# A graph network layer on one core: a step's second four gathers get one more wait, and a sign change moves to GpSimd

## Chip, core and metric

The kernel runs on 1 core of a Trainium2 chip. The metric is the device time of one execution in microseconds (us); the time of a kernel is the median of its runs. Engine names in the profile: PE is TensorE (matmul), PEld its weight loads, DVE is VectorE, ACT is ScalarE, POOL is GpSimd, SP is the engine that here only issues DMAs.

## What is computed

The reference is one message-passing layer over 6250 nodes of 128 values and 100000 edges, sorted by destination:

```python
row, col = (edge_index[0], edge_index[1])
msg_in = jnp.concatenate([node_features[row], node_features[col]], axis=-1)
h = jax.nn.relu(msg_in @ Wm1 + bm1)
h = jax.nn.relu(h @ Wm2 + bm2)
messages = h @ Wm3 + bm3
agg = jax.ops.segment_sum(messages, col, num_segments=num_nodes)
count = jax.ops.segment_sum(jnp.ones(...), col, num_segments=num_nodes)
agg = agg / jnp.clip(count, 1.0)[:, None]
node_in = jnp.concatenate([node_features, agg], axis=-1)
upd = jax.nn.relu(node_in @ Wn1 + bn1) @ Wn2 + bn2
return node_features + upd          # then layernorm(x + this)
```

## The kernel before

It has three stages, which the trace tells apart.

The preparation (to about 90 us) turns `x` and multiplies it by the two halves of `Wm1`. This gives two tables in HBM: `atab` (one row for each source node, float32, `a_table`) and `btab` (one row of three bf16 terms for each destination node, `b_table`). It works through 13 blocks of nodes; PE, ACT, POOL and SP run in the order written, and DVE from some point on too. The row `nb2` holds the second layer's bias on all partitions: POOL's queue loads it (line 190), and DVE changes its sign (line 433). Line 553 needs it so: relu(z + b) is taken as max(z, -b), with b added back later.

The edge loop (about 91 to 1630 us) takes two groups of 512 edges in each of 98 steps (`NP`). It is a software pipeline. Its order in step i on PE is:

- `turned` (line 580) transposes the sums of step i-4, and DVE's `add_up` (line 590) adds them to `acc`;
- `first_layer` of p = i-1 (lines 529 and 536) brings the gathered rows and the one-hot picked destination rows into PSUM (`ph`); ACT applies relu (line 542, four instructions);
- `sums` of step i-3 (line 561) sums messages over destinations in two banks, and ACT copies them to `part` (line 569, two instructions, `part_of`);
- `second_layer` of step i-2 (line 551) makes 32 matmuls into four banks, and DVE takes the max with `nb2` out of each (line 553, four instructions).

The PSUM pool `p2` has four banks. `turned` takes two, `sums` two, `second_layer` four, so `turned` of the next step needs the first two banks of `second_layer` freed by DVE's line 553.

The step's inputs come through a tile `rows`, of which there are two buffers. `fetch` (line 480) fills one for step i+1 while the other is in use: eight indirect gathers of 128 rows from `atab` on POOL's queue (line 488, four for each group), and eight window loads from `btab` on SP's queue (line 494). The buffer of step i+1 is that of step i-1, so the first gather waits for the end of `first_layer` of step i-1, which runs in step i. The later seven follow it in POOL's queue. The destinations `db` are loaded by ACT's queue (line 384, two DMAs a step), which stand behind the two copies of line 569 in ACT's order.

The node stage (from about 1638 us) divides by the counts, applies the last two layers and normalizes.

Of the kernel before, what the change touches and what calls it, by code (L numbers as in the profile page):

```python
# [9 lines left out]
F32 = mybir.dt.float32  # L10
# [3 lines left out]
ALU = mybir.AluOpType  # L14
# [5 lines left out]
P = 128  # L20
# [7 lines left out]
def kernel(  # L28
# [36 lines left out]
    nc = tc.nc  # L65
    N, D = x.shape
    E = src.shape[0]
    H = wm1.shape[1]
    HC = H // P
    GT = 4  # L70
# [19 lines left out]
    srcT = const.tile([P, NG, GT], I32, name="srcT")  # L90
# [51 lines left out]
    nb2 = const.tile([P, 1, H], F32, name="nb2")  # L142
# [5 lines left out]
    ld = edge.enter_context(tc.tile_pool(name="ld", bufs=4, side="right"))  # L148

    with tc.tile_pool(name="prep", bufs=1) as prep, tc.tile_pool(  # L150
        name="brow", bufs=6
    ) as brow, tc.tile_pool(name="pp", bufs=3, space=PSUM) as pp, tc.tile_pool(
        name="pb", bufs=5, space=PSUM
# [7 lines left out]
        with tc.high_priority():  # L161
# [6 lines left out]
            def load_x(b0, b1, behind=None):  # L168
                t0, t1 = 4 * b0, 4 * b1
                if behind is not None:  # L170
                    nc.vector.tensor_copy(x_sb[:, t0, :1], xT[:, behind * 4 * P:behind * 4 * P + 1])
                nc.sync.dma_start(x_sb[:, t0:t1, :].rearrange("p (b i) d -> p b i d", i=4), xb[:, b0:b1])
# [89 lines left out]
        def a_table(t0):  # L262
            m = min(2, NT - t0)
            pbt = products(t0, m, 0)
            rows = brow.tile([P, 2, H], F32, name="at", bufs=7)
            nc.scalar.copy(rows[:, :m], pbt[:, :m])
            nc.sync.dma_start(rows_of(atab, t0, m), rows[:, :m])
# [33 lines left out]
        def turn(t0):  # L301
            m = min(4, NT - t0)
            w = min(m * P, N - t0 * P)
            pt = pp.tile([P, 4 * P], F32, name="pt", tag="pp")
            for i in range(m):
                n = min(P, w)
                nc.tensor.transpose(pt[:, i * P:i * P + n], x_sb[:n, t0 + i, :], ident[:n, :n])
            nc.scalar.copy(xT[:, t0 * P:t0 * P + w], pt[:, :w])
# [97 lines left out]
        for i in range(BLOCKS):  # L406
            if i in X_LOADS:
                load_x(*X_LOADS[i], behind=i)
                if X_LOADS[i][1] == BLOCKS - 1:
                    nc.sync.dma_start(x_sb[:N - NTF * P, NTF, :], x[NTF * P:, :])  # L410
            for n, t0 in enumerate(range(4 * i, min(4 * i + 4, NT), 2)):

                if n == (i == 0) and i + 1 < BLOCKS:
                    turn(4 * i + 4)
                a_table(t0)
            b_stores()
            for _ in range(min(len(blank), 3 if i < BEHIND else 1)):
                nc.gpsimd.memset(blank.pop(0), 0.0)
            if i == BEHIND + 1:
                weights(i)  # L420
            if i == INDICES:
                starts()
            if i - INDICES in (1, 2):
                columns(i - INDICES - 1)
                partition_bases(i - INDICES - 1)
            if i == BLOCKS - 1:
                nc.scalar.copy(tilei, base[0:1].rearrange("p r w -> p (r w)"))
            if i >= BEHIND:
                b_block(i - BEHIND)
            if BLOCKS - 3 <= i:  # L430
                early.append(destinations(2 * len(early), 2, dst_row))
        assert not blank
        nc.vector.tensor_scalar(nb2, nb2, -1.0, None, op0=ALU.mult)
        behind = list(X_BEHIND)
        with tc.manual_schedule(engines={ENG.DVE}):
            for n, j in enumerate(range(BLOCKS - BEHIND, BLOCKS)):
# [27 lines left out]
    with edge, tc.tile_pool(name="wk", bufs=2) as wk, tc.tile_pool(  # L464
        name="p1", bufs=1, space=PSUM
# [11 lines left out]
        def flat_bank():  # L477
            return bank().rearrange("p t h -> p (t h)")

        def fetch(groups, queues):  # L480


            rows = ld.tile([P, 2, (GT + 1) * H], F32, name="rows", bufs=2)
            got = []
            for i, ((idx, firsts), queue) in enumerate(zip(groups, queues)):
                ag = rows[:, i, :GT * H].rearrange("p (j h) -> p j h", j=GT)
                for j in range(GT):
                    nc.gpsimd.indirect_dma_start(  # L488
                        out=ag[:, j, :], out_offset=None, in_=atab[:, :],
                        in_offset=bass.IndirectOffsetOnAxis(ap=idx[:, j:j + 1], axis=0))  # L490
                bw = rows[:, i, GT * H:].bitcast(BF16).rearrange("p (k h) -> p k h", k=2)
                for j, first in enumerate(firsts):
                    terms = btab[ds(first, WB + 1)].rearrange("n c h -> (n c) h")
                    queue.dma_start(bw[j // 2 * NQ:(j // 2 + 1) * NQ, j % 2, :], terms[:NQ])
                got.append((ag, bw))
            return got
# [69 lines left out]
        def part_of(pgs, nts):  # L566
            part = wk.tile([P, 2, H + 1], F32, name="part")
            for i, (pg, nt) in enumerate(zip(pgs, nts)):
                nc.scalar.copy(part[:nt * WN, i], pg[:nt * WN, :H + 1])  # L569
            return part  # L570
# [48 lines left out]
        NP = NG // 2  # L619
        NTS = [GT if g < NGF else LT for g in range(NG)]  # L620
        st = {}
# [6 lines left out]
        def summed(p):  # L628
            s = st[p]
            return sums([(s["ohs"][i], h2s[i], s["nts"][i]) for i in range(2)])  # L630

        rest_bank = [bank]
        rest = (x for b in X_END for x in x_part(b, lambda: rest_bank[0](), (nc.scalar, nc.scalar)))
        for i in range(NP + 4):
            if i == 8:
                late_loads()

                none = wk.tile([16, (NG * GE - E) // 16 + 1], I32, name="none", bufs=1)
                nc.vector.memset(none, NONE)
                nc.sync.dma_start(dpad[E - 16:].rearrange("(p e) -> p e", p=16), none)  # L640
                nc.sync.dma_start(dpad[:E].rearrange("(p e) -> p e", p=16), dst.rearrange("(p e) -> p e", p=16))
            if i < NP:
                dbs = early.pop(0) if early else destinations(2 * i, min(2, NGF - 2 * i), dst_row)
                if 2 * i + 1 == NGF:
                    dbs = dbs + last_destinations()
                queues = [(nc.sync, ENG.SP), (nc.scalar, ENG.Activation) if i == 0 else (nc.sync, ENG.SP)]
                firsts = [load_bases(tilei[0:1, g * GT:(g + 1) * GT], NTS[g], eng)
                          for g, (_, eng) in zip((2 * i, 2 * i + 1), queues)]
                got = fetch([(srcT[:, 2 * i + k, :], firsts[k]) for k in range(2)], [q for q, _ in queues])
                st[i] = dict(nts=NTS[2 * i:2 * i + 2], got=got, dbs=dbs)  # L650
            if i == 1:
                for k in range(SLOTS):
                    nc.gpsimd.memset(acc[:, HC, k * SLOT:(k + 1) * SLOT], 0.0)
            p = i - 1
            if p < 0:
                continue
            if p == 0:
                make_hot(0)
            k = p - 3
            if k >= 0:  # L660
                firsts = [load_bases(tilei[0:1, g * GT:(g + 1) * GT], NTS[g], ENG.DVE) for g in (2 * k, 2 * k + 1)]
                pt = turned(st[k]["part"], st[k]["nts"])
                add_up(pt, firsts, st.pop(k)["nts"])
            for step, after in enumerate((10, 12, 14)):
                if i >= after and (i - after) % 4 == 0 and (i - after) // 4 < len(pieces):
                    double((i - after) // 4, step)
            if p + 1 < NP:
                make_hot(p + 1)
            if p < NP:
                s = st[p]  # L670
                s["h1"] = first_layer(s.pop("got"), s.pop("ohts"), s["nts"])
            if p < 2:
                whole(x_part(X_FIRST[p], bank, (nc.scalar, nc.vector)))
            if p - 2 == NP - 1:
                next(rest)
            if 0 <= p - 2 < NP:
                st[p - 2]["part"] = part_of(summed(p - 2), st[p - 2]["nts"])
            if p - 2 == NP - 1:
                next(rest)
            if p - 2 == NP:  # L680
                next(rest)
            if 0 <= p - 1 < NP:
                s = st[p - 1]
                for j, nt in enumerate(s["nts"]):
                    second_layer(s["h1"][:, j], h2s[j], nt)
# [7 lines left out]
        groups = nc.values_load(  # L693
            groups_i[0:1, 0:1], min_val=0, max_val=NG,
            skip_runtime_bounds_check_because="0 or the number of groups, by its computation")
        with tc.For_i(0, groups, 1) as g:
# [3 lines left out]
            with tc.For_i(0, more, 1):  # L700
# [12 lines left out]
                got = fetch([(idx, load_bases(ti, GT, ENG.SP))], [nc.sync])  # L713
# [4 lines left out]
                part = part_of(sums([(oh, h2s[0], GT)]), [GT])  # L718
# [13 lines left out]
    with tc.tile_pool(name="nd", bufs=2) as nd, tc.tile_pool(name="nr", bufs=1) as nr, tc.tile_pool(  # L732
        name="pm", bufs=4, space=PSUM
    ) as pm, tc.tile_pool(name="pu", bufs=2, space=PSUM) as pu, tc.tile_pool(
        name="po", bufs=2, space=PSUM
# [169 lines left out]
```

## Time and profile before

| what | value |
|---|---|
| runs | 1714.18, 1715.68, 1729.71 us (median 1715.68) |
| profiled execution: its own time, its span | 1716.33 us, 1714.6 us |
| busy: PE, PEld, DVE, ACT, POOL | 1338.1, 1052.5, 656.4, 381.9, 813.5 us |
| mean granted TensorE clock | 0.855 |
| gathers, line 488 | 784, 954 ns each |
| DVE line 553 | 391, 688 ns each, 958.9 us of idle before them |
| PE line 580, idle before it | 329.9 us |
| DVE's wait before line 433 | 4.0 us, for the load of `nb2` |

The busy time of an engine is the union of its instructions; the issue of DMAs on SP and ACT is not counted. A gather on POOL counts as busy while POOL makes its descriptors; its data land later. In a group's row the duration is the mean of one instruction, and what stands behind the bar is the engine's idle time just before such instructions, with what ended most of it. "remote" stands where the profile knows no instruction that ended a wait.

### The profile page before, as it was taken

What the parts mean: (1) busy time and instruction counts of PE and PEld (TensorE: products, weight loads), DVE (VectorE), ACT (ScalarE), POOL (GpSimd) and SP (SyncE); (2) the same over time, 40 slices, a digit from 0 to 9 for tenths busy, and PEclk for the clock granted to TensorE, in tenths of its full rate; (3) what the DMA queues carried; (4) which work ended last, traced back from release to release, by engine and by line L of the source; (5) the groups of instructions that cost most, each with busy time, mean ns of one, the idle gap of its engine ahead of it and who ended that gap; (6) DMA issues with size and microseconds to landing.
All of it is one profiled execution on the core that took longest, in us unless ns stands there. A gap on an engine that the chain in (4) does not pass through costs nothing. (4 is left out here: it accounts for less than half of the span.)

```text
span 1714.6 us, 32171 instructions
## 1 busy us (share of the span) xinstructions
PE 1338.1 (78%) x11212; PEld 1052.5 (61%) x11213; DVE 656.4 (38%) x2076; ACT 381.9 (22%) x773; POOL 813.5 (47%) x873
## 2 busy tenths in 40 slices
PE   8877778677778777778777777877778778777898
PEld 7556566565666556556655665656666566655756
DVE  5523323323333333323333332333333333332467
ACT  5522112122112212212211211212222112221236
POOL 7754454454454445444445444445545444544121
PEclk9888888888887888888888788888988888888899
DMA  9743344333444334334434334333434333333133
GB/s 305 256 122 105 103 108 113 101 108 100 115 111 111 104 107 116 100 106 115 112 96 118 99 94 111 99 87 110 113 95 110 95 109 101 102 100 107 34 109 111
DMA packets 167585, 193.63 MB, mean 113 GB/s; under 512 B 30906, under 2 KB 133260, under 8 KB 167404
## 3 DMA queue, kind: packets, MB, share of 16 engines
q0 software_dynamic: 38160, 103.75, 22.4%
q1 hardware_dynamic: 100492, 61.80, 12.3%
q10 hardware_dynamic: 28768, 26.01, 5.2%
q8 instruction: 89, 1.46, 0.4%
q14 instruction: 76, 0.62, 0.1%
HBM read 168.92 MB, written 22.88 MB: 112 GB/s over the span
## 5 line engine op out<-in xcount | busy, mean ns | idle before, releaser
L488 POOL DMA_INDIRECT rows<-atab,srcT x784 | 747.7, 954 | 785.0 <-PE ph L536 568.8
L551 PE MATMUL bank<-w,h 128*128 128x256 f32 x3128 | 709.9, 385 | 1.8 <-issue 1.2
L551 PEld LDWEIGHTS bank<-w,h 128*128 128x128 f32 x3128 | 592.7, 192 | 137.2 <-PE bank L561 56.9
L553 DVE TENSOR_TENSOR h<-bank,nb 128x512 f32<-128x512 f32 x391 | 254.9, 688 | 958.9 <-remote 501.0
L542 ACT ACTIVATE h<-ph,b 128x512 f32<-128x512 f32 x392 | 236.7, 686 | 1240.3 <-PE ph L536 1199.0
L580 PE MATMUL bank<-ident,part 64*128 64x64 f32 x1173 | 103.4, 290 | 329.9 <-DVE h L553 316.8
L580 PEld LDWEIGHTS bank<-ident,part 64*128 64x128 f32 x1173 | 73.7, 184 | 376.6 <-DVE h L553 335.4
L529 PE MATMUL ph<-ident,rows 64*128 64x64 f32 x3128 | 191.3, 297 | 19.5 <-issue 18.2
L529 PEld LDWEIGHTS ph<-ident,rows 64*128 64x128 f32 x3128 | 177.8, 207 | 24.7 <-issue 22.0
L590 DVE TENSOR_TENSOR acc<-acc,bank 128x63 f32 x782 | 171.8, 220 | 35.3 <-DVE acc L590 2.1
L561 PE MATMUL bank<-h,oh 128*32 128x257 f32 x1564 | 152.3, 525 | 0.2 <-ACT x_sb L358 0.2
L536 PE MATMUL ph<-oht,rows 64*128 64x128 bf16 x1564 | 106.5, 298 | 1.0 <-DMA rows<-btab 1.0
L512 DVE TENSOR_SCALAR oht<-db,pbase 128x128 bf16<-128x128 int32 x392 | 95.0, 286 | 0.1
L536 PEld LDWEIGHTS <-rows 64*128 64x128 bf16 x1564 | 91.7, 141 | 1.2 <-DMA rows<-btab 1.2
L561 PEld LDWEIGHTS bank<-h,oh 128*32 128x32 f32 x1564 | 51.5, 140 | 54.9 <-issue 28.7
L569 ACT COPY part<-bank 128x257 f32<-128x257 f32 x196 | 66.3, 399 | 12.2 <-PE bank L561 8.4
L763 POOL TENSOR_TENSOR agg<-total,rc 128x512 f32<-128x512 f32 (+2 forms) x15 | 16.0, 1070 | 86.0 <-DMA rcol<-acc 42.0
L515 DVE TENSOR_TENSOR oh<-iota_n,dloc 128x128 f32<-128x128 f32 x196 | 55.6, 284 | 0.0
L258 PE MATMUL pbt<-w,xT 128*128 128x256 f32 x196 | 46.2, 382 | 3.5 <-DVE rest L285 3.5
L258 PEld LDWEIGHTS pbt<-w,xT 128*128 128x128 f32 x196 | 36.0, 191 | 10.0 <-DVE rest L285 4.0
L786 PEld LDWEIGHTS pot<-wu,u 128*128 128x128 f32 (+1 forms) x196 | 24.0, 191 | 6.6 <-issue 4.1
L355 PE MATMUL pxu<-xT,wu 128*128 128x512 f32 x36 | 20.6, 713 | 8.0 <-DVE rest L285 8.0
(125 smaller groups left out, 427.0 us busy)
## 6 DMA issues: line engine op xcount, KB each, us to landing
rows<-btab SPq DMA_DIRECT2D x778, 32.0 KB
db<-in_dst_dram ACTq DMA_DIRECT2D x194, 128.0 KB
rows<-atab,srcT POOLq DMA_INDIRECT x784
btab<-acc SPq DMA_DIRECT2D x24, 384.0 KB
atab<-at SPq DMA_DIRECT2D x24, 256.0 KB
xd<-in_x_dram SPq DMA_DIRECT2D x12, 256.0 KB
x2tab<-xd SPq DMA_DIRECT2D x12, 256.0 KB
x_sb<-in_x_dram SPq DMA_DIRECT2D x5, 512.0 KB
```

The source lines that it names most:

```text
L258: nc.tensor.matmul(pbt[:, a, :], xT[:, (t0 + a) * P:(t0 + a + 1) * P], w1[:, k, :], start=True, stop=True)
L488: nc.gpsimd.indirect_dma_start(out=ag[:, j, :], out_offset=None, in_=atab[:, :], in_offset=bass.IndirectOffsetOnAxis(ap=idx[:, j:j + 1], a ...
L512: nc.vector.tensor_scalar(ohts[:n, i, k, :], db[:n, k * P:(k + 1) * P], pb_cols[:n, k:k + 1], None, op0=ALU.is_equal)
L529: nc.tensor.matmul(ph[:, i, h, c, u * NQ:(u + 1) * NQ], ag[halves[h], u, c * P:(c + 1) * P], ident[halves[h], halves[h]], is_transpose=Tru ...
L536: nc.tensor.matmul(ph[:, i, h, c, k * P:(k + 1) * P], bw[halves[h], k, c * P:(c + 1) * P], ohts[halves[h], i, k, :], start=False, stop=Tru ...
L542: nc.scalar.activation(h1[:, i, c, :nh * 2 * P].rearrange("p (h e) -> p h e", h=nh), ph[:, i, :nh, c, :], AF.Relu, bias=b1[:, c:c + 1])
L551: nc.tensor.matmul(ph2[:, j - j0, :], h1[:, c, j * P:(j + 1) * P], w2[:, c, :], start=(c == 0), stop=(c == HC - 1))
L553: nc.vector.tensor_tensor(h2[:, j0:j0 + 2, :H], ph2, nb2.to_broadcast([P, 2, H]), op=ALU.max)
L561: nc.tensor.matmul(pg[j * WN:(j + 1) * WN, :H + 1], oh[:, j, :], h2[:, j, :], start=True, stop=True, skip_group_check=True)
L569: nc.scalar.copy(part[:nt * WN, i], pg[:nt * WN, :H + 1])
L580: nc.tensor.matmul(pts[h][:, i, c, :], rows, ident[halves[h], halves[h]], is_transpose=True, start=True, stop=True, skip_group_check=True)
L590: nc.vector.tensor_add(window, window, pts[h][:, i, :, k:k + WB])
```

## The change

There are two edits. The sign change of `nb2` moves from DVE, behind the preparation's blocks, to POOL, in the last block. And from step 3 on, each step allocates the next step's `rows` buffer early, behind its `part_of`, and lets ACT copy four values a partition from `part` into it: the first value of each of the four rows that the second group's gathers will write. Each of these gathers writes over one of these values, so the fifth gather of the next fetch also waits for this copy (the sixth to eighth stand behind it in the queue). The copy stands in ACT's order behind line 569 and ahead of the next two loads of `db` (line 384). On PE, DVE and SP the order of the instructions stays, but for the one that leaves DVE; there are 94 such copies, from step 3 to step 96.

```diff
             if i == BLOCKS - 1:
                 nc.scalar.copy(tilei, base[0:1].rearrange("p r w -> p (r w)"))
+                nc.gpsimd.tensor_scalar(nb2, nb2, -1.0, None, op0=ALU.mult)
...
         assert not blank
-        nc.vector.tensor_scalar(nb2, nb2, -1.0, None, op0=ALU.mult)
...
-        def fetch(groups, queues):
-            rows = ld.tile([P, 2, (GT + 1) * H], F32, name="rows", bufs=2)
+        def rows_tile():
+            return ld.tile([P, 2, (GT + 1) * H], F32, name="rows", bufs=2)
+
+        def fetch(groups, queues, rows=None):
+            rows = rows_tile() if rows is None else rows
...
+        held = None
...
-                got = fetch([(srcT[:, 2 * i + k, :], firsts[k]) for k in range(2)], [q for q, _ in queues])
+                got = fetch([(srcT[:, 2 * i + k, :], firsts[k]) for k in range(2)], [q for q, _ in queues], held)
+                held = None
...
             if 0 <= p - 2 < NP:
-                st[p - 2]["part"] = part_of(summed(p - 2), st[p - 2]["nts"])
+                part = st[p - 2]["part"] = part_of(summed(p - 2), st[p - 2]["nts"])
+                if i + 1 < NP:
+                    held = rows_tile()
+                    nc.scalar.copy(held[:, 1, :GT * H].rearrange("p (j h) -> p j h", j=GT)[:, :, :1],
+                                   part[:, 0, :GT].rearrange("p (j o) -> p j o", o=1))
```

## The prediction

> **What bounds the kernel now.** I read the page first, then the waits, then the timeline of one step, then the end of the loop, where no gathers are left. The page says that PE is busiest, but the groups show that it is not always fed:
>
> ```profile
> PE 1338.1 (78%) x11212; PEld 1052.5 (61%) x11213; DVE 656.4 (38%) x2076; ACT 381.9 (22%) x773; POOL 813.5 (47%) x873
> ...
> L488 POOL DMA_INDIRECT rows<-atab,srcT x784 | 747.7, 954 | 785.0 <-PE ph L536 568.8
> ...
> L553 DVE TENSOR_TENSOR h<-bank,nb 128x512 f32<-128x512 f32 x391 | 254.9, 688 | 958.9 <-remote 501.0
> ...
> L580 PE MATMUL bank<-ident,part 64*128 64x64 f32 x1173 | 103.4, 290 | 329.9 <-DVE h L553 316.8
> ```
>
> PE's one large idle time stands before line 580: 316.8 us over 97 waits, 3.3 us a step, for DVE's line 553. DVE is not the slow one: it sits idle itself, 501 us of it until something the profile cannot name. The timeline of a common step shows what runs then (start, duration, instruction, in brackets the idle time before it):
>
> ```profile
> 806.73 0.99 POOL L488 DMA_INDIRECT rows<-atab,srcT  x1 [6.60 <-PE ph L536]
> ...
> 808.25 7.29 PE L551 MATMUL bank<-w,h 128*128 128x256 f32 x32
> 808.84 0.39 ACT L569 COPY part<-bank 128x257 f32<-128x257 f32 x1
> 808.88 0.60 ACTq L384 DMA_DIRECT2D db<-in_dst_dram  x1
> 809.10 0.41 ACT L569 COPY part<-bank 128x257 f32<-128x257 f32 x1
> ...
> 811.78 0.95 POOL L488 DMA_INDIRECT rows<-atab,srcT  x1 [0.30 <-issue]
> 812.80 0.69 DVE L553 TENSOR_TENSOR h<-bank,nb 128x512 f32<-128x512 f32 x1 [5.50 <-PE bank L551]
> ...
> 815.53 0.95 POOL L488 DMA_INDIRECT rows<-atab,srcT  x1 [0.30 <-issue]
> 818.56 1.89 DVE L553 TENSOR_TENSOR h<-bank,nb 128x512 f32<-128x512 f32 x3 [5.06 <-remote]
> 819.30 0.90 PE L580 MATMUL bank<-ident,part 64*128 64x64 f32 x11 [3.56 <-DVE h L553]
> ```
>
> PE's 32 matmuls of line 551 are over by 815.5, the first bank's eight by 810.4. Yet DVE takes the first bank at 812.80 and the other three only at 818.56, two microseconds behind the end of the eighth gather (815.53 + 0.95 = 816.48). PE needs the first two back and stands until 819.30. At the end of the loop there are no gathers, and the same four instructions each follow their bank at once:
>
> ```profile
> 1609.66 0.69 DVE L553 TENSOR_TENSOR h<-bank,nb 128x512 f32<-128x512 f32 x1 [2.22 <-PE bank L551]
> 1611.39 0.69 DVE L553 TENSOR_TENSOR h<-bank,nb 128x512 f32<-128x512 f32 x1 [1.03 <-PE bank L551]
> ```
>
> There the step takes 10.6 us, against 16.1 us in the one above (first gather 806.73 to 822.82). So the loop is bound by a circle: first layer ends, eight gathers of 1.25 us run 9.75 us, word of PE's finished banks reaches DVE about 2 us behind them, DVE and `turned` and the next first layer take some 4.3 us, and the next gathers start. Over the 93 steps between 117.5 and 1590 us the mean from first gather to first gather is 15.84 us. 48 of them last 16.2 to 16.8; ten last 13.2 to 14.1. In the short ones the word of at least one bank got through while gathers still ran.
>
> **The change, part by part.** *The copy on ACT.* 94 copies of 128x4. The nearest row is the 128x4 square root of line 810, 292 ns; 94 x 0.292 = 27 us of ACT. They lie in ACT's idle time before line 542 (1199 us in 94 waits, 12.8 us a step), so they cost 0; without that cover 27 us. Behind the copy in ACT's queue stand the two loads of `db` (808.88 and 809.90 here). The copy waits for the second line 569, which ends at 809.51, so the first load slips by about 1 us and the second by about 0.5. DVE needs their data only at the next first layer, some 13 us on: 0.
>
> *The wait of the fifth gather.* Counted from the first gather of the step, the second copy of line 569 ends at 809.10 + 0.41 - 806.73 = 2.78 us, in nearly all steps; in the latest of them at 3.97. Add 0.3 for the new copy and some 0.2 for its own list of waits: 3.3 us, at worst 4.5. The fifth gather starts at 811.78 - 806.73 = 5.05 us. So the wait is over 1.75 us (at worst 0.5) before the gather's turn. Behind it in POOL's queue stand gathers six to eight, for which PE's first layer waits, one step later; nothing is late. Does a second wait cost POOL time by itself? In the preparation the fifth gather waits for ACT too (for the index copy), and its row shows no more than any other:
>
> ```profile
> 61.05 0.95 POOL L488 DMA_INDIRECT rows<-atab,srcT  x1 [0.30 <-issue]
> 62.31 0.95 POOL L488 DMA_INDIRECT rows<-atab,srcT  x1 [0.30 <-issue]
> ```
>
> So 0 by the nearest row. The other bound: 0.1 us a step, as the first gather's start is that much longer where it carries many waits (1.30 us to the second, not 1.25, up to 0.3 more): 94 x 0.1 = 9 us, all of it on the circle. Below nothing: a longer pause may let word of a bank through; its price stands with the rivals. I take 0.
>
> *The sign change.* On DVE it cost more than its 0.29 us, since DVE waited for the load of `nb2`, and POOL and PE behind it:
>
> ```profile
> 34.49 0.29 DVE L433 TENSOR_SCALAR nb<-nb 128x256 f32<-128x256 f32 x1 [4.04 <-DMA nb<-in_L_gnn_bm_dram]
> 34.70 1.28 DVE L285 TENSOR_TENSOR rest<-pbt,acc 128x512 f32<-128x512 f32 x2
> 35.44 1.13 PE L258 MATMUL pbt<-w,xT 128*128 128x256 f32 x4 [3.45 <-DVE rest L285]
> 35.45 1.21 POOL L294 CAST acc<-rest 128x512 bf16<-128x512 f32 x2 [3.98 <-DVE rest L285]
> ```
>
> At most 4.0 us come back. At least 0: the preparation ends with table stores and 16 gathers one behind the other from 57.15 us, whose start also waits on DMAs (0.44 us of idle, ended by a DMA). On POOL the instruction now stands among lines 294 and 298, near 55 us, ahead of these gathers; the row of a 128x256 product on POOL (line 763) has 0.73 us, a 64x196 one 0.98. Its wait for `nb2` is long over by then. From -4.0 to +1.0, I take -2.
>
> The sum against the profiled execution: span 1714.6, with 1.7 us around it 1716.3; 0 + 0 - 2 gives 1714.3. The median shown lies 0.65 below that execution, so 1713.7; I say 1714.
>
> A rule weighed: the Trainium skill, page "SBUF — State Buffer", section "Who interferes with whom", says that a DVE instruction with at most one SBUF input does not contend with GpSimd, and that PE and ACT never wait on anyone. Line 553 has one input in PSUM and one in SBUF, and still stands 5.06 us until the gathers are over. By the rule gathers and line 553 are independent, and moving the second four would be free until they miss the next first layer; by the rows each microsecond that the last gather moves is a microsecond of the step. For a wait that does not bind both give 0.
>
> **The rivals.** *A pause opens (faster).* If the fifth gather starts even some tenths later, with word of the first bank (PE done by about 3.6 us) queued, DVE may get one or two banks before the second four. For it: the short steps, 13.5 us, are those where line 553 got in early, and a pause is just what would help. Against: the wait is over before its turn. If a third of 94 steps become short: 31 x (15.84 - 13.5) = 73 us, 1641; if all, 1714 - 94 x 2.34 = 1494. From a tenth of the steps on it counts (22 us).
>
> *The wait binds and nothing gets through (slower).* Place: the fifth gather. The copy comes late (its many waits are slow on ACT, or the sums' copies wait longer for PE's word), from 5.05 us behind the first gather on. Then gathers five to eight and the word behind them move by the same amount, and the circle with them. At 0.5 us: 94 x 0.5 = +47, 1761; at 0.2 us +19, 1733. For it: the copies already hang on PE's word, which is late in this stretch. Against: 1.75 us of margin in a common step. The displaced `db` loads would act with it, since more transfers then share the time of gathers five to eight.
>
> *The steps only fall otherwise.* The step lengths scatter with 0.96 us, unrelated from one to the next; 0.96 x sqrt(94) = 9 us on the sum. That is the width of the likeliest case, and the runs' 1714 to 1730 agree.
>
> **How the numbers follow.** About 1% (17 us) is what a measurement of this kernel can tell from no change. No effect of the wait: 0.48, with its own range 1700 to 1731. Slower by the bound wait or the moved loads: 0.29, mostly 1733 to 1770. Faster by the pause: 0.23, anywhere from 1490 to 1697, half of it above 1650. Range 1650 to 1770: it leaves out about 0.11 below and 0.08 above.
>
> **What would show it.** Right: the fifth gather still 5.05 us behind the first with 0.30 us of idle, the new ACT copy ending near 3.3 us, line 580's idle near 317 us, mean step near 15.8; no wait before line 285 at 34.5 us, and the first gather some 2 us before 57.15. Wrong to the slow side: POOL's waits name ACT for tens of microseconds, and steps above 16.4. Wrong to the fast side: line 580's idle well under 250 us, with line 553 starting between 4 and 8 us behind the first gather twice in a step. A fifth gather that is late in the trace falsifies the margin, whichever way the time goes.

## The result, and the profile after

The changed kernel takes 1744.22 us (1736.54 to 1746.59) against 1715.76 us (1714.18 to 1729.71): ratio 1.0136, 95% interval 1.0101 to 1.0171. It is slower by 28 us, where no change was forecast as likeliest. The profiled execution spans 1743.9 us, 29.3 more than before.

Its page, the rows that answer to those shown of before:

```profile
PE 1347.9 (77%) x11212; PEld 1062.2 (61%) x11213; DVE 653.5 (37%) x2075; ACT 391.9 (22%) x867; POOL 815.9 (47%) x874
...
L491 POOL DMA_INDIRECT rows<-atab,srcT x784 | 749.4, 956 | 821.2 <-PE ph L539 604.2
...
L556 DVE TENSOR_TENSOR h<-bank,nb 128x512 f32<-128x512 f32 x391 | 253.0, 687 | 997.5 <-PE bank L554 472.5
...
L583 PE MATMUL bank<-ident,part 64*128 64x64 f32 x1173 | 106.1, 298 | 363.0 <-DVE h L556 352.2
```

Lines have moved by three: 491 is the gather (488 before), 556 the max (553), 583 `turned` (580). The gathers take what they took, and no releaser of theirs is ACT: GpSimd waits 604.2 us for PE's first layer (568.8 before). PE waits 352.2 us for DVE (316.8), and DVE is idle for 997.5 us before its max (958.9). All three have grown by 35 to 39 us. The circle turns more slowly, and nothing new stands in it.

The timeline of a common step after (start, duration, instruction, in brackets the idle time before it):

```profile
807.62 0.96 POOL L491 DMA_INDIRECT rows<-atab,srcT  x1 [7.21 <-PE ph L539]
...
808.70 7.17 PE L554 MATMUL bank<-w,h 128*128 128x256 f32 x32
...
809.68 0.67 ACT L572 COPY part<-bank 128x257 f32<-128x257 f32 x2
...
810.20 0.24 ACT L686 COPY rows<-part 128x4 f32<-128x4 f32 x1
...
812.64 0.95 POOL L491 DMA_INDIRECT rows<-atab,srcT  x1 [0.30 <-issue]
...
816.41 0.95 POOL L491 DMA_INDIRECT rows<-atab,srcT  x1 [0.30 <-issue]
816.52 0.69 DVE L556 TENSOR_TENSOR h<-bank,nb 128x512 f32<-128x512 f32 x1 [7.96 <-issue]
...
819.43 1.89 DVE L556 TENSOR_TENSOR h<-bank,nb 128x512 f32<-128x512 f32 x3 [2.22 <-remote]
820.17 0.90 PE L583 MATMUL bank<-ident,part 64*128 64x64 f32 x11 [2.63 <-DVE h L556]
```

The new copy takes 0.24 us and ends 2.82 us behind the first gather. The fifth gather starts at 812.64 - 807.62 = 5.02 us, with the 0.30 us of any gather. So the new wait holds no gather up. Yet DVE gets the first bank 8.90 us behind the first gather (6.07 in the step shown of before). The word it waits for is the mark that PE sets at the end of a bank. In the step shown of before, the matmuls that set the four marks end at 810.37, 812.09, 813.82 and 815.54, and the trace has the marks themselves at 812.78, 818.53, 818.63 and 818.72: what is late is the mark, before DVE. (The profile models the ends of matmuls, but PE had gone on to the first matmul of `turned` by 815.48.)

I measured each step from first gather to first gather, for the same 93 steps in both traces:

| | before | after |
|---|---|---|
| sum of 93 steps, us | 1472.7 | 1509.3 |
| rest of the span, us | 241.9 | 234.6 |
| steps under 15 us (their mean) | 15 (13.91) | 4 (14.19) |
| steps of 15 to 16 us | 17 | 7 |
| steps from 16 us on (their mean) | 61 (16.39) | 82 (16.36) |
| steps in which the first max starts before the fifth gather | 26 | 7 |
| start of the fifth gather, mean | 5.071 | 5.067 |

The loop loses 36.6 us, the rest gains 7.3. The mean step goes from 15.84 to 16.23 us, but a long step is as long as it was. What is gone is the short steps, those in which word of a bank slipped through while gathers ran.

### The profile page after: what moved, and what is told of

Same layout as the page of the kernel before. It is cut to its first block, busy times and chain, and to the rows that moved or that the text cites. A ratio compares the mean times of both kernels' runs of the same rounds, so it can differ in the third digit from the quotient of the medians.

```text
span 1743.9 us, 32767 instructions
## 1 busy us (share of the span) xinstructions
PE 1347.9 (77%) x11212; PEld 1062.2 (61%) x11213; DVE 653.5 (37%) x2075; ACT 391.9 (22%) x867; POOL 815.9 (47%) x874
## 5 line engine op out<-in xcount | busy, mean ns | idle before, releaser
L491 POOL DMA_INDIRECT rows<-atab,srcT x784 | 749.4, 956 | 821.2 <-PE ph L539 604.2
L556 DVE TENSOR_TENSOR h<-bank,nb 128x512 f32<-128x512 f32 x391 | 253.0, 687 | 997.5 <-PE bank L554 472.5
L583 PE MATMUL bank<-ident,part 64*128 64x64 f32 x1173 | 106.1, 298 | 363.0 <-DVE h L556 352.2
L532 PEld LDWEIGHTS ph<-ident,rows 64*128 64x128 f32 x3128 | 182.0, 214 | 10.7 <-issue 8.6
L564 PE MATMUL bank<-h,oh 128*32 128x257 f32 x1564 | 156.1, 536 | 0.2 <-ACT x_sb L358 0.2
L796 PE MATMUL pot<-wu,u 128*128 128x128 f32 (+1 forms) x196 | 24.4, 276 | 1.4 <-ACT u L784 1.4
```

The lines of the kernel that those rows point to most:

```text
L491: nc.gpsimd.indirect_dma_start(out=ag[:, j, :], out_offset=None, in_=atab[:, :], in_offset=bass.IndirectOffsetOnAxis(ap=idx[:, j:j + 1], a ...
L532: nc.tensor.matmul(ph[:, i, h, c, u * NQ:(u + 1) * NQ], ag[halves[h], u, c * P:(c + 1) * P], ident[halves[h], halves[h]], is_transpose=Tru ...
L556: nc.vector.tensor_tensor(h2[:, j0:j0 + 2, :H], ph2, nb2.to_broadcast([P, 2, H]), op=ALU.max)
L564: nc.tensor.matmul(pg[j * WN:(j + 1) * WN, :H + 1], oh[:, j, :], h2[:, j, :], start=True, stop=True, skip_group_check=True)
L583: nc.tensor.matmul(pts[h][:, i, c, :], rows, ident[halves[h], halves[h]], is_transpose=True, start=True, stop=True, skip_group_check=True)
L796: nc.tensor.matmul(pot[:r, i, :], u[:, c, i * P:i * P + r], wu2[:, c, :], start=(c == 0), stop=(c == HC - 1))
```

## The experiments

Jobs landed on several chips. In two of them the kernel before took 1155 to 1157 us, in the others 1667 to 1720, and on one chip 1673 in one job and 1720 in another. (The two at 1155 to 1157 us met the same chip.) So each ratio is against the kernel before in the same job, and jobs are compared only roughly. In the texts on record T1 is "the copy holds back the `db` loads", T2 "the fifth gather's second wait itself costs", T3 "the earlier start of the loop costs", T4 or N "any further ACT instruction among the gathers costs"; L, S and H came later: "the lists of waits" (what an instruction must wait for before it starts), "SP's first window load comes 0.10 us later", "GpSimd's queue gets the second four gathers later".

**Parts of the change where PE's word is prompt.** Four kernels in one job: the sign change alone, the copy alone, and two with both where the copy stands elsewhere or writes elsewhere.

```diff
 # e3: behind the db loads in ACT's order, in the next step
-                    held = rows_tile(); nc.scalar.copy(held[...], part[...])   # ahead of destinations()
+                    held = rows_tile(); nc.scalar.copy(held[...], part[...])   # behind destinations()
 # e4: the same place, a tile of its own
-                    held = rows_tile()
-                    nc.scalar.copy(held[:, 1, :GT * H]..., part[:, 0, :GT]...)
+                    spare = wk.tile([P, GT, 1], F32, name="spare")
+                    nc.scalar.copy(spare, part[:, 0, :GT]...)
```

> The kernel before with the sign change on GpSimd alone; no copy, no second wait. The first gather of the changed kernel came 2.06 us earlier and the loop's later steps some 7 us earlier than before, so the theories that put the loss into the copy or its wait (T1, T2, T4) expect 1707 to 1714 us, steps of 15.8 us and 15 or so steps below 15 us. T3, that the shifted start of the loop is what takes the short steps away, expects about 1744 us and 4 short steps.

> The changed kernel with the sign change back on DVE: the ACT copy and the fifth gather's wait alone. T1, T2 and T4 expect 1745 to 1755 us (the loss without the gain ahead of the loop) and a mean step of 16.2 us. T3 expects 1716 us.

> The changed kernel, but the ACT copy stands behind the step's two db loads in ACT's order instead of ahead of them; the fifth gather waits for it all the same. T1 (the copy holds back the db loads by about 1 us, into the stretch in which SP issues the last window loads and PE's word is slow) expects the loss gone: 1707 to 1716 us, first db issue spread from 0.9 to 2.3 us behind the first gather again. T2 (the second wait on GpSimd's queue itself closes the gap between the fourth and the fifth gather) and T4 (any further instruction on ACT in this stretch) expect 1740 to 1750 us. If the db loads are slow themselves the copy may end behind 5.05 us, and then the fifth gather is late: that would show as ACT in GpSimd's waits.

> The changed kernel, but the ACT copy, at its place ahead of the db loads, writes a small tile of its own, so no gather waits for it. T1 and T4 expect the loss to stay: 1738 to 1750 us, mean step 16.2 us. T2 expects it gone: 1707 to 1716 us.

Before took 1156.93 us here. Sign change alone: 1151.75, ratio 0.9954 (0.9938 to 0.9970). Copy alone: 0.9992 (0.9979 to 1.0005). Both, copy behind the `db` loads: 0.9958 (0.9942 to 0.9973); copy elsewhere: 0.9954 (0.9938 to 0.9970). All steps last 10.06 us, which is eight gathers of 1.257 us. The timeline of a step (sign change alone) shows why nothing else counts:

```profile
599.75 0.99 POOL L488 DMA_INDIRECT rows<-atab,srcT  x1 [0.30 <-issue]
...
601.08 0.69 DVE L553 TENSOR_TENSOR h<-bank,nb 128x512 f32<-128x512 f32 x1 [0.56 <-PE bank L551]
...
602.81 0.69 DVE L553 TENSOR_TENSOR h<-bank,nb 128x512 f32<-128x512 f32 x1 [1.03 <-PE bank L551]
...
604.81 0.95 POOL L488 DMA_INDIRECT rows<-atab,srcT  x1 [0.30 <-issue]
606.15 0.58 PE L580 MATMUL bank<-ident,part 64*128 64x64 f32 x12
606.26 0.69 DVE L553 TENSOR_TENSOR h<-bank,nb 128x512 f32<-128x512 f32 x1 [1.03 <-PE bank L551]
```

Gathers run without a break, and DVE takes each bank as PE ends it, 1.72 us apart. So the copy, its waits and the fifth gather's second wait cost next to nothing in themselves: gathers back to back would show 0.1 us a step as 9 us. What the change costs where the kernel before takes 1716 us does not show here at all, so T1 to T4 stay open; that the cost goes through the late word is so far a conclusion from the difference.

> The same kernel once more (the copy behind the db loads, the fifth gather waiting for it all the same), because the runs so far were on a chip on which the kernel before took 1157 us and not 1716. Where the kernel before takes about 1716 us: T1 (the db loads held back by the copy) expects the loss gone, 1705 to 1716 us and some 15 steps below 15 us; T2 (the second wait on GpSimd's queue) and T4 (any further ACT instruction in this stretch) expect 1735 to 1750 us and about 4 short steps. Where it takes 1157 us: 0.996 of it again, with all steps at 10.06 us, and nothing is told apart.

That run met the same chip: 0.9964 (0.9944 to 0.9985), nothing told apart.

**The `db` loads earlier.**

```diff
+                early.append(destinations(2 * i + 2, ...))   # behind first_layer, ahead of part_of
```

> The kernel before with the sign change on GpSimd, no copy, and the two db loads of a step ahead of the two copies of line 569 in ACT's order (behind line 542) instead of behind them: the opposite of what the change did to them. Where the kernel before takes about 1716 us: T1 (what counts is when the db loads are issued) expects more short steps than 15, and 1640 to 1705 us; T2 and T4 expect no effect beyond the sign change, 1707 to 1716 us. Where it takes 1157 us: about 1151 us, since a step there is eight gathers of 1.257 us and nothing else.

1776.13 us against 1667.02: 1.0649 (1.0478 to 1.0820). T1 read backwards promised a gain; this is a large loss, in two runs, with 30 steps under 15 us and others of 20 us and more. The moment of two DMA issues can move the loop by more than the change did; no theory had forecast this, and why it does was not followed up.

**The changed kernel and its parts in one job, before at 1671.08 us.** The last of the four has no copy into `rows`; its `db` loads stand at the end of the step and wait for the step's last max.

```diff
 # e8
+            if behind is not None:
+                nc.scalar.copy(db[:, 0, :1], behind)          # behind = h2s[1][:, GT - 1, :1]
```

> The changed kernel itself, as the measure for the next three on one chip. Where the kernel before takes 1650 us or more, all theories expect about 1.014 of it, as on the first chip. Where it takes 1157 us: about 0.996 of it.

> The copy behind the db loads in ACT's order, the fifth gather still waiting for it. Where the kernel before takes 1650 us or more: T1 (the db loads are held back by the copy into a stretch in which they disturb SP's issues and PE's word) expects the loss gone, 0.992 to 1.000 of before; T2 (the second wait on GpSimd's queue) and T4 (any further ACT instruction in this stretch) expect 1.01 to 1.02. Where it takes 1157 us: 0.996 again.

> The copy at its place ahead of the db loads, but into a small tile of its own, so no gather waits for it. Where the kernel before takes 1650 us or more: T1 and T4 expect the loss to stay, 1.01 to 1.02 of before; T2 expects it gone, 0.992 to 1.000. Where it takes 1157 us: 0.996 again.

> The kernel before with the sign change on GpSimd and no copy into rows; the db loads of the next step stand at the end of a step instead, behind a small ACT copy that waits for the last line 553, so they are issued when no gathers run. Where the kernel before takes 1650 us or more: if db loads that are issued among the gathers are what delays PE's word (T1 in its general form), the steps become short: 13 to 14 us, 1450 to 1560 us; if gathers and SP's window loads do that by themselves, nothing changes but scatter, 0.98 to 1.02 of before. Where it takes 1157 us: 0.996, steps of 10.06 us.

| kernel | ratio to before | steps under 15 us of 93 |
|---|---|---|
| changed kernel | 1.0345 (1.0293 to 1.0398) | 6 |
| copy behind the `db` loads | 1.0257 (1.0222 to 1.0292) | 7 |
| copy elsewhere | 1.0019 (0.9983 to 1.0055) | 27 |
| no copy into `rows`, `db` loads late | 0.9991 (0.9956 to 1.0026) | 29 |

The page of the changed kernel in this job:

```profile
L583 PE MATMUL bank<-ident,part 64*128 64x64 f32 x1173 | 105.1, 294 | 356.2 <-DVE h L556 340.9
```

and of the copy that writes a tile of its own:

```profile
L583 PE MATMUL bank<-ident,part 64*128 64x64 f32 x1173 | 98.0, 278 | 275.0 <-DVE h L556 258.6
```

T1 falls: with the `db` loads held back just as long (2.62 and 3.29 us behind the first gather, the median in both), but nothing written into `rows`, the loss is gone (PE's wait 258.6 instead of 340.9 us), and with the loads ahead of the copy most of it stays. T4 falls too: the copy elsewhere has the further ACT instruction. T3 falls as well: the last two kernels have the sign change on GpSimd. That change gave 5 us where it was measured alone, so as much may hide in their two ratios. The cause sits in the writing into `rows`; whether it is the fifth gather's wait, as T2 has it, is the next question.

**The fifth gather's wait taken away, or over early.** In the first, `rows` is four floats wider and the copy writes only these. In the second the copy stands ahead of line 542 and is over 0.3 us behind the first gather at the latest.

```diff
 # e9_copy_beside
-            return ld.tile([P, 2, (GT + 1) * H], F32, name="rows", bufs=2)
+            return ld.tile([P, 2, (GT + 1) * H + GT], F32, name="rows", bufs=2)
+                    nc.scalar.copy(held[:, 1, (GT + 1) * H:], part[:, 0, :GT])
 # e9_wait_early, in first_layer, ahead of the relu
+                nc.scalar.copy(held[:, 1, :GT * H]...[:, :, :1], b23[:, :1]...to_broadcast([P, GT, 1]))
```

> The changed kernel, but the rows tile is four floats wider and the ACT copy writes these four, which no gather and no window load writes: the copy, its place and its list of waits stay, SP's and the first gather's waits on ACT for the use two steps back too; only the fifth gather's wait for this step's copy is gone. Where the kernel before takes 1650 us or more: T2 (the fifth gather's wait is the cause) expects the loss gone, 0.99 to 1.005 of before, and some 25 steps below 15 us; if ACT's list of waits or SP's longer list is the cause, 1.02 to 1.035 as in the changed kernel. Where it takes 1157 us: 0.996.

> The fifth gather waits for an ACT copy into its rows as in the changed kernel, but the copy (of the values of a constant) stands ahead of line 542 instead of behind line 569, so it is over within 0.3 us of the first gather's start and not at 2.8 us. Where the kernel before takes 1650 us or more: if the cost comes from GpSimd's queue being held at the fifth gather until 2.8 us (in the kernel before all eight gathers are handed over when the first starts, in the changed one the second four at 2.85 us), the loss is gone or small, 0.99 to 1.01; if a second wait by itself costs, whenever it is over, 1.02 to 1.035. Where it takes 1157 us: 0.996 to 1.000.

Before took 1676.45 us. Copy beside: 1.0758 (1.0722 to 1.0793), with no wait of the fifth gather at all. Wait early: 1.0445 (1.0405 to 1.0485). T2 falls. I had taken the gather's wait for the only thing that writing into `rows` adds. It adds more: with a new writer of the buffer, other queues wait for ACT too, and what an instruction does not wait for itself is read by instructions ahead of it in its queue, two waits in each (ACT's list of 13 is six of these, 0.04 us each, and the copy's own wait). In the traces, behind the end of the first layer (medians):

| kernel | first gather | SP's first window load | SP's eighth ends | first max |
|---|---|---|---|---|
| before (first job) | 0.27 | 0.03 | 7.00 | 6.26 |
| copy elsewhere | 0.27 | 0.03 | 6.20 | 4.81 |
| changed kernel (first job) | 0.27 | 0.13 | 8.59 | 7.90 |
| changed kernel (second) | 0.27 | 0.13 | 7.85 | 7.61 |
| wait early | 0.27 | 0.13 | 8.58 | 9.07 |
| copy beside | 0.74 | 0.13 | 9.82 | 9.06 |

In all slow ones of this table SP's first window load comes 0.10 us later; PE's end, the last thing to come, is there read by an instruction ahead of the load and no longer by the load itself. In the copy beside the first gather carries the wait for ACT as well and comes 0.47 us later. By the steps that would be 94 x 0.47 = 44 us of its 125, and its long steps do last 16.90 us in the mean, 0.5 more than in the first job's kernel before. So this kernel has a further loss of its own, and what it shows is only that a loss needs no wait of the fifth gather.

**Number of instructions, or lists of waits.** Six more ACT copies without a wait; the window loads in a tile of their own, which shortens SP's list from 11 waits to 2 and the first gather's from 9 to 2; and the same with the change's copy.

```diff
 # e10_six_more, on the copy elsewhere
+                    for k in range(7):
+                        nc.scalar.copy(spare[:, k, :], part[:, 0, k * GT:(k + 1) * GT])
 # e10_windows_apart (and with the copy of the change)
-                bw = rows[:, i, GT * H:].bitcast(BF16)...
+            wins = ld.tile([P, 2, H], F32, name="wins", bufs=2)
+                bw = wins[:, i, :].bitcast(BF16)...
```

> The copy into a small tile of its own (which cost nothing so far) seven times over: six more ACT instructions among the gathers of each step, without a wait, and the db loads held back by some 1.2 us more. Where the kernel before takes 1650 us or more: N (each further instruction among the gathers holds up PE's word and SP's issues, whatever it is) expects 1.02 to 1.04 of before; L (it is the lists of waits, ACT's own or those that SP and GpSimd carry since the copy writes into rows) expects 0.99 to 1.01. Where it takes 1157 us: 0.996.

> The kernel before with the sign change on GpSimd and no copy; the window loads go into a tile of their own (wins, two buffers, the same room as before), so SP's first window load of a step waits for 2 semaphores instead of 11, and the first gather for 2 instead of 9. Where the kernel before takes 1650 us or more: if lists of waits that are read among the gathers are what delays (L), this is faster than before, 0.93 to 0.98; if not, 0.99 to 1.00 by the sign change alone. Where it takes 1157 us: 0.996.

> The changed kernel with the window loads in a tile of their own: the ACT copy, its list (9 waits instead of 13) and the fifth gather's wait stay, SP waits for ACT no more. Against the kernel with the windows apart and no copy: if ACT's list or the fifth gather's wait is the cause, 1.02 to 1.035 again; if SP's longer list is the cause, the same time within 0.7%. Where the kernel before takes 1157 us: 0.996 of it.

Before took 1716.57 us. Six more: 1.0031 (0.9997 to 1.0066), so N falls. Windows apart: 1.0664 (1.0603 to 1.0725) by the upper three of its four runs, 1821 to 1839 us, and 1.04 by the fourth, 1791 us, the one profiled; slower by either, where L expected faster. With the copy: 1503.66 us, 0.8783 (0.8733 to 0.8834), a value that no theory had named. Shorter lists move the first gather from 0.27 us behind the end of the first layer to 0.18 ahead of it. A step with the windows apart and no copy:

```profile
559.27 0.94 POOL L489 DMA_INDIRECT rows<-atab,srcT  x1 [7.09 <-PE ph L530]
559.36 1.07 PE L562 MATMUL bank<-h,oh 128*32 128x257 f32 x16
...
564.64 0.38 ACT L570 COPY part<-bank 128x257 f32<-128x257 f32 x1 [2.68 <-PE bank L552]
...
571.17 0.37 ACT L570 COPY part<-bank 128x257 f32<-128x257 f32 x1 [6.15 <-remote]
571.26 1.89 DVE L554 TENSOR_TENSOR h<-bank,nb 128x512 f32<-128x512 f32 x3 [9.43 <-remote]
```

PE ends the sums at 560.43, but ACT copies the second bank only at 571.17. The gathers are now ahead of that word too. With the copy, the fifth gather really waits (179.8 us for ACT's copy in 85 waits; it starts 6.70 us behind the first in the mean): it hangs on `part`, `part` hangs on the late word, and so the gathers pause until the word is through. That the pause gives more than it costs is so far a reading of one trace; the next run tests it.

**A pause on purpose, and SP's first load put back.**

```diff
 # e11_pause, in second_layer, at the second bank of line 551, ahead of line 553; no copy behind part_of
+                if held is not None and j0 == 2:
+                    nc.scalar.copy(held[:, 1, :GT * H]...[:, :, :1], ph2[:, 0, :GT]...)
 # e11_sp_first, behind the copy of the change
+                    nc.scalar.copy(held[NQ:, 1, (GT + 1) * H - 1:], part[NQ:, 0, :1])
```

> The changed kernel, and a second small ACT copy behind the first that writes one value in the place of the step's eighth window load. SP's eighth load now waits for ACT (long over by its turn), and SP knows of the copies by then, so the first load of a later step has no wait for ACT any more: its list is that of the kernel before. The copy, its list and the fifth gather's wait stay. Where the kernel before takes 1650 us or more: S (SP's first window load 0.10 us later is the cause) expects SP's first load at 0.03 us again and the loss gone, 0.99 to 1.005 of before; L (ACT's list of 13 waits among the gathers is the cause) expects 1.02 to 1.045. Where it takes 1157 us: 0.996.

> The changed kernel, but the ACT copy that the fifth gather waits for reads the second bank of line 551 instead of part: PE is done with that bank some 5.2 us behind the first gather, so the wait binds in every step. Where the kernel before takes 1650 us or more: if a real pause lets PE's word through (the forecast's fast rival), the fifth gather starts near 6.6 us, line 553 takes its first three banks between 5.9 and 8.3 us, the step is 13.2 to 13.7 us and the time 1450 to 1520 us (0.86 to 0.90); if gathers five to eight are merely 1.5 us later (the slow rival), 94 x 1.5 = 141 us more, 1.08. Where it takes 1157 us, a step is eight gathers, and the wait can only cost: 1.00 to 1.06.

Before took 1672.88 us. With SP's first load back at 0.03 us the changed kernel still has 1.0212 (1.0148 to 1.0276): S does not explain the loss; it may be a part. The pause, which is fast, has SP's first load at 0.13 us all the same. The pause gives 1487.28 us, 0.8883 (0.8832 to 0.8934). All 93 steps are short, 13.47 us in the mean; the fifth gather starts at 6.77 us in the mean. One of them:

```profile
583.77 0.94 POOL L491 DMA_INDIRECT rows<-atab,srcT  x1 [2.19 <-PE ph L539]
...
587.58 0.95 POOL L491 DMA_INDIRECT rows<-atab,srcT  x1 [0.30 <-issue]
590.08 2.48 DVE L559 TENSOR_TENSOR h<-bank,nb 128x512 f32<-128x512 f32 x4 [4.08 <-PE bank L554]
590.22 0.17 ACT L557 COPY rows<-bank 128x4 f32<-128x4 f32 x1 [3.67 <-PE bank L554]
...
590.65 0.95 POOL L491 DMA_INDIRECT rows<-atab,srcT  x1 [2.12 <-ACT rows L557]
591.53 0.58 PE L586 MATMUL bank<-ident,part 64*128 64x64 f32 x12
```

The fourth gather's record ends at 588.53. At 590.08 to 590.22, 1.6 us later, word of two banks reaches DVE and ACT together; DVE then takes all four without a break. `turned` follows PE's second layer with no wait of PE for DVE (352.2 us of it in the changed kernel). The gathers stood for 2.12 us (2.03 in the mean), and the mean step is some 2.9 us shorter than a long one of before or after.

**What is left of the loss.** ACT's list with only the eighth gather held, SP's first load as before (the edit is against the run with SP's first load put back).

```diff
-                    nc.scalar.copy(held[:, 1, :GT * H]...[:, :, :1], part[:, 0, :GT]...)
+                    nc.scalar.copy(held[:, 1, (GT - 1) * H:(GT - 1) * H + 1], part[:, 0, :1])
```

> As the run with SP's first load restored, but the first ACT copy writes one value, in the row of the eighth gather alone: gathers one to seven are handed over together, only the eighth is held until 2.8 us (its turn is at 8.8 us). ACT's list of 13 waits, its place and SP's lists stay. Where the kernel before takes 1650 us or more: L (ACT's list among the gathers is what is left of the loss) expects 1.015 to 1.03 of before; H (the hand-over of the second four at 2.85 us) expects 0.99 to 1.007. Where it takes 1157 us: 0.996.

Before took 1720.14 us, this 1737.05: 1.0102 (1.0065 to 1.0138), with 5 steps under 15 us. That is between the two bands. The changed kernel itself was 1.0136 in one job and 1.0345 in another, so this leaves H little room and does not prove L. It also has a loss in which the fifth gather waits for no copy.

So it is shown that the loss comes from writing into `rows` (1.0345 against 1.0019 in one job), and that ACT's time, the number of its instructions and the delay of the `db` loads are not it. Two kernels have a loss without the fifth gather's wait, so that wait is not needed for one. How the loss divides between ACT's list of 13 waits, SP's later first load and the hand-over of the second gathers stays open.

## Why the forecast was wrong, step by step

- *The circle*: right, and it is what the loss runs through. Word of PE's banks comes late while gathers run, and a step is long or short by whether one slips out. It left out PE's granted clock, which is 0.84 in the loop (200 to 1000 us) and 1.00 over the first 55 us: in the long steps the first layer takes 2.84 us, against 1.61 where the clock stays at 1.00. Its "about 2 us behind the last gather" holds in the median: the second max starts 11.80 us behind the first gather before and 11.93 after; the eighth gather's record ends near 9.8.
- *The copy on ACT*: 0.23 us each in the mean and nothing by itself (0.9992 where the word is prompt). It ended at 2.82 us, earlier than 3.3. The `db` loads it holds back were priced 0, and within the noise that stands (1.0019 with the copy elsewhere).
- *The fifth gather's wait*: the margin was right, 5.067 us against 5.071 and 0.30 us of idle. The step that failed is the one drawn from it: "nothing is late" and "So 0 by the nearest row", with 94 x 0.1 = 9 us as the worst. In its place the loop lost 36.6 us, and in another job writing into `rows` cost 56 us (1732.15 against 1676.08 us with the same copy into a tile of its own). The step asked which gather waits, and not which other queues get a longer list because `rows` has a new writer. SP's first load and ACT's copy did; which of them costs how much stays open. The nearest row also came from the preparation, where gathers run one behind the other and no line 553 waits behind them.
- *The steps only fall otherwise*: 0.96 x sqrt(94) = 9 us was the width of the likeliest case. It took the share of short steps for chance around a fixed mean. That share is what the change moved: 15 to 4 steps under 15 us, 11 x some 2.45 = 27 us, and 10 fewer of 15 to 16 us, some 8 more, of 36.6 in all.
- *The sign change*: taken at -2, at best -4.0; it gave that best or more. The first gather comes at 55.09 us instead of 57.15, as said, and the third step's first gather at 84.13 instead of 91.17; in the other kernels with the sign change on GpSimd that run at 1490 to 1830 us it comes at 83.96 to 89.25, so the 7 us are in part scatter. DVE's 4.0 us of waiting is gone (PE's line 258 now waits 0.8 us in all). Alone it gave 5.2 us at 1157 us (3.5 to 7.2 by the interval, which still holds 4.0). The bound looked no further than the first gather; what comes back behind it was not traced.
- *The wait binds*: 1733 to 1770 holds the result, but by luck: the place was wrong. No gather was late.
- *A pause opens*: it did not in the changed kernel, for the reason given, that the wait is over before its turn. As a mechanism it was right: "if all, 1494" assumed 13.5 us a step, and a wait that binds gave 13.47 us and 1487 us (in a job in which before took 1673).
- *The rule weighed*: the Trainium skill, page "SBUF — State Buffer", section "Who interferes with whom", has DVE with one SBUF input free of GpSimd, and PE and ACT waiting on nobody. It speaks of SBUF's ports, and there the rows agree in both: the max takes 0.69 us at 1157 us and at 1716 us. What is late at 1716 us is its start (7.96 us of idle before the first max above, 1.03 between maxima at 1157 us). So the prediction took the rule too far when it read from it that gathers and line 553 are independent.

## What to carry to other kernels

A tiny write into a shared buffer costs little as an instruction; list every queue that touches the buffer later and see whose list of waits grows, and whether it is read where the loop is tight. Where a loop's steps come in two lengths, forecast the share of each, since that share is not noise. And where finished work is told late under a stream of gathers, a short stop of that stream, tied to the very work that is waited for, can be worth more than it costs: with 2.0 us of stop a step the kernel took 185.6 us less, some 2.0 us a step or 11%. That was on a chip where the word is late; where it is prompt the pause was not run.

## What the hardware showed unexpectedly

The same kernel ran at 1157 us in two jobs on one chip and at 1667 to 1720 us in the rest. In the first, PE's word reached DVE at once under running gathers (a max every 1.72 us); in the others it came in most steps only about 2 us behind the last gather. The gathers themselves were alike (953 and 954 ns). The granted clock differs as well: it is 1.00 over the first 55 us in every trace, then (200 to 1000 us) 1.00 in the five kernels at 1150 to 1156 us, 0.82 to 0.87 in the slower ones, and 0.90 and 0.95 in the two whose gathers pause. On one chip it was 0.85 with SP's first load put back and 0.90 with the pause, so at least a part of it goes with PE's waiting. Nor is it PE's word alone that is held up: SP's register moves ahead of its window loads, which wait for nothing, take 0.03 us in the median in both, but up to 1.14 us in the first job's kernel before and at most 0.04 in the sign change alone at 1152 us. Why is open: no run here separates the causes. It was also unexpected that a first gather 0.45 us earlier and one 0.47 us later both went with 4 to 8% more time: -0.18 us with the windows apart (1.04 to 1.07), 0.74 us with the copy beside (1.0758), against 0.27 us; both kernels differ in more than that.
